# A decoder layer on one core: ScalarE's order in the expert steps, and who does the last sums and scalings

## The chip, the core and the metric

The kernel runs on one core of one Trainium2 chip. The core has TensorE (matrix products, results in PSUM), VectorE, ScalarE and GpSimd (elementwise work of different kinds), and SyncE, which does no arithmetic and issues transfers. Each engine runs its own queue in order; semaphores tie them. The metric is the device time of one execution in microseconds (us), taken as the median of several runs. Before the change it is 984.56 us (three runs, 982.49 to 984.77).

## The reference

A decoder layer in float32 with a layer norm behind each of three parts. The input has 8 sequences of 112 tokens with 512 features, so 896 tokens or seven tiles of 128.

```python
x = _layernorm(x + attn(x))             # causal self-attention, 16 heads of 128
x = _layernorm(x + xattn(x, ctx_2048))  # gated linear attention to 375 context rows
x = _layernorm(x + ffn(x))              # mixture of experts

# ffn: 8 experts, each token goes to its best two
logits = h @ router_weight.T + router_bias
top_vals, top_idx = jax.lax.top_k(logits, 2)
top_w = softmax(top_vals)
gate_up = h @ gate_up_proj + gate_up_proj_bias     # per expert, 512 -> 2 x 512
gate = minimum(gate_up[..., ::2], 7.0); up = clip(gate_up[..., 1::2], -7.0, 7.0)
act = (up + 1.0) * gate * sigmoid(1.702 * gate)
expert_out = act @ down_proj + down_proj_bias      # per expert, 512 -> 512
out = sum over the token's two experts of top_w * expert_out
```

## The kernel before

The first two thirds of the span (self-attention and cross-attention) are not touched. The change lies in the experts' part, the last `with` block, which starts near 740 us.

**Tokens in blocks.** The router (`route`) writes every token twice, once for each of its two experts, into an array `store` in memory, sorted by expert; `list_blocks` works out from the counts which expert and which block of `store` each of 18 steps gets. A step s takes a block of 128 rows (`xblk`, four buffers). Steps 0 to 4 have one expert each; steps 5 to 12 are paired, with 64 rows for each of two experts; steps 13 to 17 are again single. Weights lie in four lanes of three 1 MB slabs (gate, up, down). SyncE fetches the weights of a coming step when TensorE has released the slab, and skips the transfer where the lane already has that expert.

**A step in engines.** The loop over s at the end of the kernel issues, in an order written out by hand (`tc.manual_schedule` keeps the queues of TensorE, VectorE, ScalarE and SyncE as written), three stages at once:
- `project(s, st, 0)` and `project(s, st, 1)`: TensorE multiplies the turned block bT(s) by the gate and the up weights into PSUM (`gups`, L1143). VectorE adds the bias and clips (L1151, L1153, L1158). ScalarE computes the sigmoid of the gate (L1155). VectorE joins them to the gated block (L1159, L1162).
- `transposed_block` for aT(s-1) and, in `start(s + 1)`, for bT(s+1): TensorE turns the gated block of the step before and the token block of the step after into PSUM (L1040), ScalarE copies each into SBUF (L1044). `start` also has VectorE derive the per-row scalars (L1052 to L1078).
- `down(s - 1)`: TensorE multiplies aT(s-1) by the down weights (`yps`, L1170), and VectorE adds the result to a begun result y (L1181), which GpSimd scatters to an array `parts` in memory (L1183).

The begun result comes from `begin_result(s)`: ScalarE scales the down bias by the row's score (L1201) and the token block by a flag that says whether this is the row's first expert (L1202), GpSimd adds the two (L1203). The bias was spread over the partitions by VectorE's shuffle (`spread_biases`, L995) after a transfer that ScalarE issues (`fetch_biases`, L987). In the kernel before, shuffle and `begin_result(s + 1)` stand at the end of step s.

**The end.** A token's two results meet in two ways. For tiles of tokens, `close_tiles` adds the two halves read back from `parts` (L1235), takes layer-norm statistics, one root for all seven (`closing_roots`, L223 to L225), and scales each tile (`closing_scale`) before SyncE writes it out (L1244). The rows of the last five steps (`LATE` = 5, steps 13 to 17) come too late for that: each gathers the partner rows from `parts` into `sums` (L1210), adds its own result (`add_own`, L1206), is normed by `close_steps`, and is scattered into the output over the rows written before (`write`, L1220); `find_again` finds rows of which both halves fall into these steps. In the kernel before, `close_steps` takes steps 13 to 16 together and then step 17 alone, inside `finish`. `tick` and `settle` move `close_tiles` and the last tile's router work (`close`) along between the steps. L243 is the root of that tile's earlier layer norm, L530 and L533 its turning and copy for the router, L1265 the product in `find_again`.

Of the kernel before, what the change touches and what calls it, by code (L numbers as in the profile page):

```python
# [19 lines left out]
P = 128  # L20
# [40 lines left out]
def decoder_layer(ctx: ExitStack, tc: tile.TileContext, t_in: dict, out: bass.AP):  # L61
# [1058 lines left out]
    with tc.tile_pool(name="moe", bufs=2, reuse_waits="tile") as moe:  # L1120
# [17 lines left out]
        def project(s: int, st, k: int):  # L1138

            ps = bank(f"gups_{s}_{k}")  # L1140
            for c in range(C):
                for rows_, q in parts_of(s):
                    nc.tensor.matmul(  # L1143
                        ps[rows_],
                        st["bT"][:, c, rows_],
                        slab[3 * q + k][:, c, :],
                        start=(c == 0),
                        stop=(c == C - 1),
                    )
            a = moe.tile([P, I], F32, tag=f"gu{k}", name=f"gu_{s}_{k}", bufs=2 - k)  # L1150
            nc.vector.tensor_add(a, ps, st["bias"][:, k * I : (k + 1) * I])  # L1151
            if k == 0:
                nc.vector.tensor_scalar_min(a, a, LIMIT)  # L1153
                sg = moe.tile([P, I], F32, tag="sg", name=f"sg_{s}", bufs=1)
                nc.scalar.activation(sg, a, AF.Sigmoid, scale=ALPHA)  # L1155
                st["g"], st["sg"] = a, sg
            else:
                nc.vector.tensor_scalar(a, a, LIMIT, -LIMIT, ALU.min, ALU.max)  # L1158
                nc.vector.scalar_tensor_tensor(  # L1159
                    st["g"], st["g"], st["score"], st["sg"], ALU.mult, ALU.mult  # L1160
                )
                nc.vector.scalar_tensor_tensor(  # L1162
                    st["g"], a, 1.0, st["g"], ALU.add, ALU.mult
                )

        def down(s: int, st):
            ps = bank(f"yps_{s}", "aux")
# [34 lines left out]
            nc.scalar.activation(y, st["x"][:, :D], AF.Copy, scale=st["first"])  # L1202
            nc.gpsimd.tensor_add(y, y, bias)  # L1203

        def add_own(st):
            nc.vector.tensor_add(st["sum"], st["sum"], st["y"])  # L1206

        def gather(st):
            st["sum"] = sums[:, st["late"] * D : (st["late"] + 1) * D]
# [22 lines left out]
        def close_tiles():  # L1232
            for t in range(NT):
                engine = nc.vector if t < 4 else nc.gpsimd
                engine.tensor_add(xn[:, t, :], xn[:, t, :], seconds[:, t, :])  # L1235
                closing_stats(t, xn[:, t, :])
                if t in (1, 2):
                    yield
            yield
            closing_roots(0, NT)  # L1240
            yield
            for t in range(NT):
                closing_scale(t, xn[:, t, :], True)
                nc.sync.dma_start(out=out[t * P : (t + 1) * P, :], in_=xn[:, t, :])  # L1244

        def close_steps(*several, by_act=False):
            late = [(NT + s - (STEPS - LATE), steps[s]) for s in several]
# [35 lines left out]
        def finish(ps, st):  # L1283
            before_ = steps[STEPS - 2]
            nc.tensor.matmul(ps, st["same"], before_["y"], start=False, stop=True)
            nc.vector.tensor_add(st["sum"], st["sum"], ps)
            close_steps(STEPS - 1)

        def fetch_next(s: int, fetch):

# [8 lines left out]
        for s in range(STEPS + 1):  # L1299
            st = steps[s] if s < STEPS else None  # L1300
            before_ = steps[s - 1] if s else None
            if s == 0:
                spread_biases(0)
                begin_result(0)
            if st:
                project(s, st, 0)
                if s == 0:
# [1 line left out]
                    chains.append(close(NT - 1))  # L1309
                if s < STEPS - 1:  # L1310
                    tick()
            if s == STEPS:
                add_own(steps[s - 2])
            if before_:
                before_["aT"] = transposed_block(f"aT_{s - 1}", before_["g"], moe, "aT")
            if s == STEPS - 1:
                tick()
            if s == STEPS:
                settle(0)
                close_steps(*range(STEPS - LATE, STEPS - 1), by_act=True)  # L1320
            if s + 1 < STEPS:
                steps.append(start(s + 1, moe, "bT"))
                if s + 2 < STEPS:
                    fetch_biases(s + 2)
                if s + 1 > STEPS - LATE:
                    nc.vector.tensor_scalar_mul(diag, ident, keys[:, s + 1 : s + 2])
                if s == 2:
                    settle(0)
# [13 lines left out]
                find_again(s + 1)  # L1342
            if s + 1 < STEPS:
                spread_biases(s + 1)
                begin_result(s + 1)
            if s == STEPS - 1:
                settle(0)
                for late in steps[STEPS - LATE : STEPS - 2]:
                    add_own(late)

                add_own(st)
            if before_:
                down(s - 1, before_)
                if s == STEPS - 3:
                    chains.append(close_tiles())
                if s != STEPS - 3:
                    tick()
                if s == PAIRED:
                    for t in range(NT):
                        for k, to in ((1, xn), (0, seconds)):  # L1360
                            nc.sync.dma_start(
                                out=to[:, t, :],
                                in_=parts[k * T + t * P : k * T + (t + 1) * P, :],
                            )
                fetch_next(s - 1, fetch_down)
                if s + 3 < STEPS:
                    ahead_x.append(fetch_tokens(s + 3))
# [61 lines left out]
```

## Time and profile before

| | us |
|---|---|
| median of three runs | 984.56 |
| profiled execution, its own time | 981.93 |
| its span | 980.3 |
| TensorE busy | 921.4 (94%) |
| VectorE busy | 498.6 (51%) |
| ScalarE busy | 253.1 (26%) |
| GpSimd busy | 202.4 (21%) |

The profile is of one execution. Its lines are of several kinds. A timeline line gives start and duration in us, engine, line of the kernel, operation, tiles (out<-in) and shapes; brackets at its end give how long the engine stood before it and what released it. PE is TensorE, PEld its weight load, DVE VectorE, ACT ScalarE, POOL GpSimd, SP SyncE. In a line of the waits the three numbers are the total, how often, and the longest. Idle time of an engine that nobody waits for costs nothing.

### The profile page before, as it was taken

What the parts mean: (1) busy time and instruction counts of PE and PEld (TensorE: products, weight loads), DVE (VectorE), ACT (ScalarE), POOL (GpSimd) and SP (SyncE); (2) the same over time, 40 slices, a digit from 0 to 9 for tenths busy, and PEclk for the clock granted to TensorE, in tenths of its full rate; (3) what the DMA queues carried; (4) which work ended last, traced back from release to release, by engine and by line L of the source; (5) the groups of instructions that cost most, each with busy time, mean ns of one, the idle gap of its engine ahead of it and who ended that gap; (6) DMA issues with size and microseconds to landing.
All of it is one profiled execution on the core that took longest, in us unless ns stands there. A gap on an engine that the chain in (4) does not pass through costs nothing.

```text
span 980.3 us, 11063 instructions
## 1 busy us (share of the span) xinstructions
PE 921.4 (94%) x3915; PEld 467.8 (48%) x3915; DVE 498.6 (51%) x1116; ACT 253.1 (26%) x434; POOL 202.4 (21%) x264
## 2 busy tenths in 40 slices
PE   7998999999999999999999999997978799999974
PEld 3455644466445654654555455453444343334431
DVE  1356511145313551556421757666758755556685
ACT  1133311033102230322222233332214222222223
POOL 3133300031101221202002212221102422222152
PEclk9999999999999999999999999999969899999997
DMA  9995004102011001030100111113337899768953
GB/s 341 358 344 198 1 1 171 43 0 87 0 43 43 1 1 43 7 118 26 32 1 1 32 43 44 54 55 126 147 150 291 275 365 343 270 208 318 404 203 139
DMA packets 35063, 130.48 MB, mean 133 GB/s; under 512 B 3862, under 2 KB 8022, under 8 KB 25152
## 3 DMA queue, kind: packets, MB, share of 16 engines
q1 hardware_dynamic: 29296, 114.01, 32.1%
q0 software_dynamic: 4768, 14.98, 4.5%
q10 hardware_dynamic: 944, 0.79, 0.3%
q8 instruction: 31, 0.51, 0.2%
q14 instruction: 24, 0.20, 0.1%
HBM read 122.02 MB, written 30.06 MB: 155 GB/s over the span
## 4 chain that ended last, share of the span: by engine, by line
PE 78%; DVE 13%; issue 3%; ACT 3%; POOL 1%; DMA 1%; ACTq 0%; POOLq 0%; DVEq 0%
PE gups L1143 10%; PE ops L261 10%; PE vps L351 6%; PE yps L1170 5%; PE zps L459 3%; PE xqps L895 2%; PE xgps L895 2%; DVE z L868 2%; PE sps L411 2%; PE xops L261 2%; PE pps L451 1%; DVE p L436 1%; PE sumps L830 1%; PE aT_ps L1040 1%; DVE kf L790 1%
## 5 line engine op out<-in xcount | busy, mean ns | idle before, releaser
L1143 PE MATMUL gups<-slab,bT 128*64 128x512 f32 (+1 forms) x416 | 132.7, 601 | 0.0
L261 PE MATMUL ops<-slab,zT 128*128 128x512 f32 x224 | 97.9, 593 | 0.0
L1170 PE MATMUL yps<-slab,aT 128*64 128x512 f32 (+1 forms) x208 | 70.9, 624 | 10.6 <-ACT aT L1044 10.6
L1143 PEld LDWEIGHTS gups<-slab,bT 128*64 128x64 f32 (+1 forms) x416 | 47.8, 159 | 68.4 <-issue 68.3
L299 POOL TENSOR_TENSOR ws<-slab 128x256 f32<-128x256 f32 x16 | 11.7, 730 | 281.4 <-PE qk_5c L315 83.0
L261 PEld LDWEIGHTS ops<-slab,zT 128*128 128x128 f32 x224 | 42.0, 190 | 50.3 <-issue 49.5
L351 PE MATMUL vps<-slab,x0T 128*112 128x512 f32 x128 | 58.7, 613 | 1.0 <-DVE x0T L211 0.8
L1151 DVE TENSOR_TENSOR gu<-gups,biases 128x512 f32<-128x512 f32 x36 | 24.8, 689 | 62.8 <-PE gups L1143 62.8
L1170 PEld LDWEIGHTS yps<-slab,aT 128*64 128x64 f32 (+1 forms) x208 | 25.7, 167 | 49.7 <-issue 37.0
L268 DVE TENSOR_TENSOR xn<-xn,ops 128x512 f32<-128x512 f32 x28 | 19.2, 685 | 55.2 <-PE ops L261 55.2
L466 DVE COPY zT<-zps 128x448 f32<-128x448 f32 x32 | 20.0, 624 | 39.8 <-PE zps L459 39.8
L459 PEld LDWEIGHTS zps<-pT,v 112*128 112x128 f32 x256 | 33.5, 192 | 12.3 <-issue 11.2
L351 PEld LDWEIGHTS vps<-slab,x0T 128*112 128x112 f32 x128 | 22.9, 184 | 31.4 <-issue 29.7
L435 DVE TENSOR_REDUCE nm<-p 112x4 f32<-112x448 f32 x32 | 19.7, 615 | 30.6 <-POOL p L425 30.6
L261 PE MATMUL xops<-slab,gate 128*128 128x512 f32 x56 | 27.3, 633 | 7.1 <-DVE gate L870 7.1
L459 PE MATMUL zps<-pT,v 112*128 112x112 f32 x256 | 33.4, 273 | 0.0
L587 POOL DMA_INDIRECT store<-xn,rows x14 | 14.0, 1003 | 83.9 <-DVE count L627 60.1
L995 DVE STREAM_SHUFFLE biases<-biases 128x1024 f32<-128x1024 f32 (+1 forms) x28 | 29.8, 1099 | 0.0
L1183 POOL DMA_INDIRECT parts<-y,nums x16 | 16.8, 1049 | 60.9 <-DVE y L1181 44.6
L419 ACT ACTIVATE p<-sps 112x448 f32<-112x448 f32 x32 | 17.4, 544 | 45.6 <-PE sps L411 45.6
L411 PE MATMUL sps<-k,q 128*112 128x112 f32 x256 | 28.0, 262 | 0.0
L437 ACT ACTIVATE p<-p 112x448 f32<-112x448 f32 x32 | 18.4, 576 | 35.4 <-DVE p L436 35.4
(814 smaller groups left out, 1664.3 us busy)
## 6 DMA issues: line engine op xcount, KB each, us to landing
slab<-in_wg_dram SPq DMA_DIRECT2D x26, 1024.0 KB
slab<-in_wu_dram SPq DMA_DIRECT2D x26, 1024.0 KB
slab<-in_wd_dram SPq DMA_DIRECT2D x26, 1024.0 KB
store<-slab SPq DMA_DIRECT2D x8, 1806.0 KB
cT<-in_ctxT_dram SPq DMA_DIRECT2D x8, 750.0 KB
slab<-in_wq_dram SPq DMA_DIRECT2D x4, 1024.0 KB
slab<-in_wk_dram SPq DMA_DIRECT2D x4, 1024.0 KB
slab<-in_wo_dram SPq DMA_DIRECT2D x4, 1024.0 KB
```

The lines of the kernel that those rows point to most:

```text
L261: nc.tensor.matmul(ps, aT[:, c, t * P : (t + 1) * P], w[:, c, :], start=(c == 0), stop=(c == C - 1),)
L351: nc.tensor.matmul(ps[:S, :], xT[:, c, b * S : (b + 1) * S], w[:, c, :], start=(c == 0), stop=(c == C - 1),)
L411: nc.tensor.matmul(ps[:S, i * S : (i + 1) * S], qk["q"][:, rows], qk["k"][:, rows], start=True, stop=True,)
L435: nc.vector.tensor_reduce(nm, p, AX.X, ALU.max, negate=True)
L459: nc.tensor.matmul(zps[:, i * S : (i + 1) * S], v[:, half * 4 + i, hl * DH : (hl + 1) * DH], pT[:, i * S : (i + 1) * S], start=True, stop= ...
L466: nc.vector.tensor_copy(zT[:, hl, half * HALF : (half + 1) * HALF], zps[:, :HALF])
L868: nc.vector.reciprocal(zf, zf)
L895: nc.tensor.matmul(ps[:, :HALF], w[:, c, g * P : (g + 1) * P], xT[:, c, cols], start=(c == 0), stop=(c == C - 1),)
L995: nc.vector.stream_shuffle(b, b, [0] * XH)
L1143: nc.tensor.matmul(ps[rows_], st["bT"][:, c, rows_], slab[3 * q + k][:, c, :], start=(c == 0), stop=(c == C - 1),)
L1151: nc.vector.tensor_add(a, ps, st["bias"][:, k * I : (k + 1) * I])
L1170: nc.tensor.matmul(ps[rows_], st["aT"][:, c, rows_], slab[3 * q + 2][:, c, :], start=(c == 0), stop=(c == C - 1 and s < STEPS - 1),)
```

## The change

It has four parts.
1. In step s, ScalarE's copies of aT(s-1) and bT(s+1) are issued first, then the sigmoid (in a function of its own, `gate_sigmoid`), then `begin_result(s)`, which moves from the end of step s-1 into step s.
2. Of the late sums, those of steps 13 to 15 go to GpSimd; those of 16 and 17 stay on VectorE. They are issued after the down product of the step, and the sum of step 16 comes in step 17.
3. Of the seven tile scalings, the first three go to VectorE and four stay on ScalarE, and the generator `close_tiles` yields at other points, so that the root and the scalings come after step 17's second product.
4. `close_steps` takes steps 13 to 15 together, scaled by ScalarE, and in `finish` steps 16 and 17 together, scaled by VectorE.

```diff
             if k == 0:
                 nc.vector.tensor_scalar_min(a, a, LIMIT)
-                sg = moe.tile([P, I], F32, tag="sg", name=f"sg_{s}", bufs=1)
-                nc.scalar.activation(sg, a, AF.Sigmoid, scale=ALPHA)
-                st["g"], st["sg"] = a, sg
+                st["g"] = a
...
+        def gate_sigmoid(s: int, st):
+            sg = st["sg"] = moe.tile([P, I], F32, tag="sg", name=f"sg_{s}", bufs=1)
+            nc.scalar.activation(sg, st["g"], AF.Sigmoid, scale=ALPHA)
...
-        def add_own(st):
-            nc.vector.tensor_add(st["sum"], st["sum"], st["y"])
+        def add_own(st, engine=nc.vector):
+            engine.tensor_add(st["sum"], st["sum"], st["y"])
...
             yield
             closing_roots(0, NT)
-            yield
             for t in range(NT):
-                closing_scale(t, xn[:, t, :], True)
+                closing_scale(t, xn[:, t, :], t > 2)
                 nc.sync.dma_start(out=out[t * P : (t + 1) * P, :], in_=xn[:, t, :])
+                if t == 2:
+                    yield
+                    yield
...
             nc.vector.tensor_add(st["sum"], st["sum"], ps)
-            close_steps(STEPS - 1)
+            close_steps(STEPS - 2, STEPS - 1)
...
             if s == 0:
                 spread_biases(0)
-                begin_result(0)
...
-            if s == STEPS:
-                add_own(steps[s - 2])
             if before_:
                 before_["aT"] = transposed_block(f"aT_{s - 1}", before_["g"], moe, "aT")
-            if s == STEPS - 1:
-                tick()
+            if s + 1 < STEPS:
+                steps.append(start(s + 1, moe, "bT"))
+            if st:
+
+                gate_sigmoid(s, st)
+                begin_result(s)
             if s == STEPS:
                 settle(0)
-                close_steps(*range(STEPS - LATE, STEPS - 1), by_act=True)
+                close_steps(*range(STEPS - LATE, STEPS - 2), by_act=True)
             if s + 1 < STEPS:
-                steps.append(start(s + 1, moe, "bT"))
                 if s + 2 < STEPS:
                     fetch_biases(s + 2)
...
             if s + 1 < STEPS:
                 spread_biases(s + 1)
-                begin_result(s + 1)
+            if before_:
+                down(s - 1, before_)
             if s == STEPS - 1:
-                settle(0)
                 for late in steps[STEPS - LATE : STEPS - 2]:
-                    add_own(late)
+                    add_own(late, nc.gpsimd)
+                add_own(before_)

                 add_own(st)
             if before_:
-                down(s - 1, before_)
                 if s == STEPS - 3:
                     chains.append(close_tiles())
```

## The prediction

> **What bounds the kernel now.** I read the shares of the span first, then the waits of TensorE from 740 us on, then the timeline around each wait, then busy time and DMA share by stretch.
>
> ```profile
> PE 921.4 (94%) x3915; PEld 467.8 (48%) x3915; DVE 498.6 (51%) x1116; ACT 253.1 (26%) x434; POOL 202.4 (21%) x264
> ```
>
> TensorE sets the time, so an edit pays only where TensorE stands, or after its last matmul. From 740 us on it stands at five places. The timeline of TensorE alone gives them, with the wait and its releaser in brackets:
>
> ```profile
> 746.87 0.63 PE L530 MATMUL x2T_ps<-ident,xn 128*128 128x128 f32 x4 [2.93 <-DVE is_first L1054]
> 774.63 6.17 PE L1170 MATMUL yps<-slab,aT 128*128 128x512 f32 x8 [6.92 <-ACT aT L1044]
> 940.18 0.46 PE L1265 MATMUL keys<-sums,allones 128*128 128x128 f32 x2 [1.99 <-DVE sums L1326]
> 954.35 6.77 PE L1170 MATMUL yps<-slab,aT 128*128 128x512 f32 x8 [2.96 <-ACT aT L1044]
> 962.28 3.70 PE L1170 MATMUL yps<-slab,aT 128*128 128x512 f32 x8 [0.73 <-ACT aT L1044]
> ```
>
> The largest (6.92 us) ends with ScalarE's copy of a turned block. Its cause stands in the timeline of 758 to 785 us:
>
> ```profile
> 763.24 0.60 PE L1040 MATMUL aT_ps<-ident,gu 128*128 128x128 f32 x4
> ...
> 770.52 0.72 ACT L1201 ACTIVATE more_biases<-more_biases,score 128x512 f32<-128x512 f32 x1 [10.73 <-DVE more_biases L995]
> ...
> 772.09 1.60 DVE L1054 TENSOR_TENSOR is_first<-xblk,es 128x1 f32<-128x1 f32 x1
> 772.18 1.28 ACT L1155 ACT_TABLE_LOAD   x1 [0.33 <-DVE gu L1153]
> ...
> 774.01 0.57 ACT L1044 COPY aT<-aT_ps 128x512 f32<-128x512 f32 x1
> ...
> 775.76 0.69 DVE L1162 SCALAR_TENSOR_TENSOR gu<-gu,gu 128x512 f32<-128x512 f32 x1
> ```
>
> The block was turned in PSUM at 763.84. ScalarE stood for 10.73 us in front of a bias scaling that waits for a VectorE shuffle, then did two scalings, a table load and a sigmoid, and only then the copy. The stall also costs clock, as busy time by stretch shows (five pairs of busy time and count, then granted clock, share of the transfer engines, GB/s):
>
> ```profile
> 760.00:780.00 20.00, 13.08 (x31) 5.86 (x30) 17.08 (x68) 5.54 (x8) 7.16 (x10) 0.83 0.78 261
> 780.00:800.00 20.00, 20.00 (x60) 9.64 (x59) 8.88 (x23) 4.52 (x8) 6.48 (x8) 1.00 1.01 383
> 800.00:860.00 60.00, 60.00 (x277) 22.16 (x277) 34.44 (x79) 14.63 (x25) 16.22 (x19) 1.00 0.87 299
> 860.00:903.00 43.00, 42.95 (x197) 16.68 (x194) 24.14 (x62) 11.70 (x20) 11.49 (x12) 1.00 0.71 265
> ```
>
> In the trace's clock rows half clock stood from 773.4 to 780.2 and from 954.3 to 961.1: straight after the stalls of 6.92 and 2.96 us, so that eight matmuls took 6.17 and 6.77 us where they take 3.43 elsewhere.
>
> The end is set otherwise:
>
> ```profile
> 967.63 1.03 POOL L1220 DMA_INDIRECT out_dram<-sums,places  x1 [11.19 <-ACT sums L232]
> ...
> 973.08 0.99 POOL L1220 DMA_INDIRECT out_dram<-sums,places  x1 [0.30 <-issue]
> ```
>
> Five scattered writes leave GpSimd 1.35 us apart from the moment the first late sum is scaled; landing and closing take from 974.07 to 980.3.
>
> **The change, part by part.** s is the step; gate(s) and up(s) are its two products.
>
> *Order on ScalarE.* It was: bias scaling and result start of s (waiting for the shuffles that end step s-1), sigmoid(s), copy aT(s-1), copy bT(s+1), bias transfers. It becomes: both copies, sigmoid, the two scalings, transfers. No instruction is added, and one table load less is issued.
>
> (a) Around 744 us. The last tile's root (L243, at 745.65) stood behind the sigmoid's table load of step 0. Now its own load comes first, without a wait, on an idle engine, and it runs when its variance is there (VectorE's aggregate ends 743.59): 2.0 us earlier. TensorE waited 2.93 us for that tile. Its copy (L533) is now behind bT, load, sigmoid and two scalings: 743.95 + 0.57 + 1.28 + 0.63 + 0.72 + 0.71 = 747.9, done at 748.5, and TensorE needs it at 748.9, after gate(1). That product hides it; uncovered, each us costs one. I take 1.9.
>
> (b) The stall at 774. aT(1) is copied as soon as it is turned, so the down product follows up(2) at once: at 765.6 (767.5 less the 1.9 of (a)). It ends 769.1 at full clock, gate(3) at 772.5. What is late next is VectorE, which makes the block for the following turn. Its L1162 ended at 776.45: 1.9 earlier by (a), and 0.8 by L1054, which took 1.60 us beside GpSimd's begun result instead of 0.15. (1.45 would be won, but then the sigmoid, whose load still starts with L1153's end at 772.11 and which ends 1.99 later, comes last.) So the turn starts at 773.75 instead of 784.08: 6.92 + 2.74 (clock) + 1.9 - a new wait of 1.25 = **10.3 us**.
>
> The rule on this in the Trainium skill ("TensorE: Matmul & The Clock Gate", section "HAM oscillation — how this bites in real kernels") is to avoid idle gaps above about 3.4 us. By it the new waits of about 1 us are free and so would be waits of 3 us. The row says otherwise: 2.96 us at 954 was enough for half clock, while 2.93 us at 746 was not. By the rule a later stall of 3 us costs 3; by the row up to 3 + 3.2. I take the rule for waits near 1 us, and keep the row for the range.
>
> (c) What a faster TensorE triggers. The weights of the paired steps were loaded in a stream that is nearly full: share 1.01 and then 0.87 in the rows above (780 to 860 us: 383 and 299 GB/s). In the trace's transfer records 1 MB blocks followed one another every 3.4 us while they queued. Counting by 3.4 from the first one after the lists (771.23, now 769.2), the twentieth, a down weight of step 7, lands at 769.2 + 19 x 3.4 + 3.7 = 837.5. It was needed at 846.12; 10.3 us earlier is 835.8: late by 1.7. Its neighbours are met within 1 us. Bounds: at 3.2 us per block nothing is late; at 3.5 (from 808 to 827 us the pace was 3.6) it is 3.6, and with half clock behind it 6.8. I take **-2**: the pace of the longer stretch, and two short waits rather than one. From step 10 on most pair weights are skipped (share 0.71) and no further debt arises.
>
> Bias transfers are issued some 0.9 us later in the step, behind two scalings of 0.72 and 0.71 (the copies start about 0.5 earlier). SyncE waits for their landings (17.4 us in three waits at L962), so weights start up to 0.9 later; the smallest lead there, 3.0 us (down weight of step 8: landed 854.6, needed 857.6), covers it.
>
> (d) The end, with the times of before. GpSimd's result start no longer meets VectorE's L1153 (0.84 us beside it, 0.43 otherwise): VectorE, and with it the keys product, 0.4 earlier. aT(16) is copied at once: the stall of 2.96 and the half clock behind it (6.77 for 3.43) go, and the product before the last ends at 954.6. But VectorE's last gated block is ready only at 955.3 (its first add, behind the tiles' statistics, at 951.6, then 0.67 + 0.43 + 0.68 + 0.43 + 0.74 + 0.69), and its copy now stands behind sigmoid, two scalings, load and root: 953.4 + 0.7 + 0.7 + 1.28 + 0.3 = 956.4, done 957.0. The last product then ends at 960.7 instead of 966.0. Only part of that reaches the end, since VectorE goes on: block ready 955.3, root's two small steps until 956.9, three tile scalings x 0.55 (L234's row) = 958.6, result and two sums x 0.68 = 960.7, three statistics x 0.8 = 963.1, root and two small ones 963.9, ScalarE's first scaling 964.7. First write 964.7 instead of 967.63; the last two sums, closed in a pair, are ready by 968.2, before the fourth write at 968.8. All five writes move together: **3.0 us**, the 0.4 included.
>
> The two sums that wait on GpSimd: 1.28 us each (L1235's row there) against 0.69 on VectorE. Its four gathers end at 956.0, so sums and last start are done by 959.9 and VectorE needs them at 960.0. A rule speaks against this: "GPSIMD Engine Reference", section "Engine selection", keeps two-input elementwise work on VectorE, as GpSimd is about twice slower; the rows agree (1.28 to 0.69), but by the rule this costs 1.8 us more, by the timeline nothing as long as GpSimd only waits. Bounds 0 to 2 (its port meets VectorE's statistics).
>
> The scalings moved to VectorE take 3 x 0.55 from it and give ScalarE 3 x 0.72; counted above. The order on SyncE's queue is unchanged. GpSimd now writes parts of s-1 before it starts s: up to 2.7 us earlier for step 12's, hidden.
>
> Sum: 10.3 - 2 + 3.0 = 11.3. The profiled execution has a span of 980.3 and 981.93 in all; it would become 969.0 and 970.6. The median of the runs, 984.56, lies 2.6 above it: **973.3**.
>
> **Rivals.**
> 1. *The weights become the wait.* For: share 1.01. A late block of 3.6 us with half clock behind it takes 6.8 instead of 2: gain 6.5, 978.1. Against: the share of 0.87 and 0.71 after 800.
> 2. *The end gives nothing*: GpSimd's sums or the root ahead of the last copy hold VectorE by 3 us. Gain 8.3, 976.3. Against: GpSimd stands 11.19 us before the writes.
> 3. *No change*: the shift is eaten whole before step 9 and the end gives nothing. 984.5. Against: three stalls are removed in three places.
> 4. *Slower: ScalarE blocked by its bias transfers.* A transfer waits for the one that used its semaphore before, often a weight (a wait of 6.2 us at L1201 is put down to such a one). Now scalings and triggers stand directly ahead of the next copy. From a trigger to the next copy are 7.8 us, and the copy has 2.8 us of lead (843.36 + 0.57 against 846.12, and 0.6 earlier): blocking above 10.6 us stops TensorE. Over 13 steps it eats 11.3 from 11.5 us per step; at 12.5 per step it is -24.7 + 11.3: 998. Against: the longest such wait is 6.2.
>
> **How the numbers follow.** Forecast 0.60 (973.3, its own range 970 to 976), rival 1 0.18, rival 2 0.08, rival 3 0.05, rival 4 0.09. A measurement of this kernel tells some 0.3% (3 us) from nothing. Faster 0.86, same 0.05, slower 0.09. Range 969 to 979: no late block and the end as counted is 971.3, less some 2 for the spread of the runs; above, rival 1 and 1 us.
>
> **What would show it.** (a) The root at about 743.7. (b) The down product near 765.6 without half clock behind it, the turn near 774; if aT is copied early and the turn still starts after 780, the VectorE step is wrong. (c) Waits of TensorE for weights between 815 and 850, together near 2 us; above 4 rival 1 holds. (d) Last product about 5 us nearer to the one before, first write 3 us earlier against TensorE's step 17. Waits of ScalarE for transfers above 10 us would mean rival 4.

## The result, and the profile after

The changed kernel takes 978.37 us (median; 977.49 to 980.17) where the kernel before takes 983.72 on the same chip (982.49 to 984.77): ratio 0.9948, 95% interval 0.9933 to 0.9963. It is 5.35 us faster. (The 984.56 given ahead is the median of three of the five runs of the kernel before.) The forecast was 973.3, a gain of 11.3: the sign is right, and the gain is a little under half of what was summed.

The profiled execution has a span of 976.5 us (before: 980.3). The part of the program in front of 738 us is the same in both, and in this execution it happens to end 1.3 us later (first product of the last cross-attention output at 737.79 instead of 736.47). So 1.3 is added below wherever a time after is set against one before. Line numbers are those of the changed kernel; behind L1155 they are shifted (GpSimd's addition in the begun result, L1203, is L1205 now, the late sums L1208, the tile additions L1237).

The timeline of TensorE from 738 us on, with its waits, of the changed kernel (start, duration, in brackets the wait and what ended it):

```profile
746.05 0.63 PE L530 MATMUL x2T_ps<-ident,xn 128*128 128x128 f32 x4 [0.79 <-DVE is_first L1054]
774.98 0.63 PE L1040 MATMUL aT_ps<-ident,gu 128*128 128x128 f32 x4 [1.22 <-DVE gu L1160]
824.34 3.22 PE L1143 MATMUL gups<-slab,bT 128*64 128x512 f32 x13 [1.21 <-DMA slab<-in_wu_dram]
840.58 3.65 PE L1172 MATMUL yps<-slab,aT 128*64 128x512 f32 x14 [0.21 <-DMA slab<-in_wd_dram]
935.14 0.77 PE L1269 MATMUL keys<-sums,allones 128*128 128x128 f32 x2 [2.52 <-DVE sums L1330]
952.34 3.70 PE L1172 MATMUL yps<-slab,aT 128*128 128x512 f32 x8 [0.68 <-ACT aT L1044]
957.79 1.12 PE L1289 MATMUL yps<-y,sums 128*128 128x512 f32 x2 [1.75 <-DVE y L1183]
```

The waits of 6.92 at 774 and 2.96 at 954 are gone, the one at 746 has shrunk from 2.93 to 0.79. New are two waits for weights (824 and 840), a longer one at the `keys` product (2.52, before 1.99), and one of 1.75 before the last product. Where the old stall stood, the timeline of all engines after shows:

```profile
763.05 0.58 ACT L1044 COPY aT<-aT_ps 128x512 f32<-128x512 f32 x1 [4.09 <-PE aT_ps L1040]
766.72 3.60 PE L1172 MATMUL yps<-slab,aT 128*128 128x512 f32 x8
...
771.39 1.28 ACT L1166 ACT_TABLE_LOAD   x1 [7.27 <-DVE gu L1153]
772.69 0.63 ACT L1166 ACTIVATE sg<-gu 128x512 f32<-128x512 f32 x1
```

ScalarE copies aT at 763.05, straight after the turning, and the down product follows at 766.72 in 3.60 us, at full clock. Busy time by stretch (the columns are those of the prediction):

```profile
760.00:780.00 20.00, 18.78 (x56) 9.01 (x56) 17.57 (x71) 6.81 (x11) 7.73 (x10) 1.00 0.81 287
...
800.00:860.00 60.00, 58.58 (x268) 22.24 (x264) 31.50 (x71) 12.61 (x23) 16.05 (x19) 1.00 0.89 324
...
925.00:951.00 26.00, 23.48 (x62) 10.95 (x61) 23.93 (x51) 6.32 (x10) 12.15 (x11) 0.93 0.54 194
```

In 800 to 860 TensorE now has 58.58 of 60 us, with the transfers at 0.89 of their time. In 925 to 951 VectorE has 23.93 of 26 and hardly a gap, while TensorE waits and runs part of its time at half clock (0.93). What it does there and just behind, beside GpSimd:

```profile
928.45 0.99 POOL L1185 DMA_INDIRECT parts<-y,nums  x1 [0.86 <-DMA seconds<-parts]
929.07 1.95 DVE L1153 TENSOR_SCALAR gu<-gu 128x512 f32<-128x512 f32 x1
929.45 1.28 POOL L1237 TENSOR_TENSOR xn<-xn,seconds 128x512 f32<-128x512 f32 x1
...
951.90 2.50 POOL L1208 TENSOR_TENSOR sums<-sums,y 128x512 f32<-128x512 f32 x2
951.91 3.73 DVE L225 SCALAR_TENSOR_TENSOR closing<-closing 128x7 f32<-128x7 f32 x1
954.34 1.27 POOL L1205 TENSOR_TENSOR y<-y,biases 128x512 f32<-128x512 f32 x1
955.68 1.46 DVE L234 TENSOR_SCALAR xn<-xn,closing 128x512 f32<-128x512 f32 x3
...
963.99 1.03 POOL L1222 DMA_INDIRECT out_dram<-sums,places  x1 [8.38 <-ACT sums L232]
...
969.25 0.98 POOL L1222 DMA_INDIRECT out_dram<-sums,places  x1 [0.30 <-issue]
```

Two lines of the kernel before, for comparison:

```profile
936.95 1.26 DVE L1235 TENSOR_TENSOR xn<-xn,seconds 128x512 f32<-128x512 f32 x1
...
956.17 0.17 DVE L225 SCALAR_TENSOR_TENSOR closing<-closing 128x7 f32<-128x7 f32 x1
```

L225 works on 128x7 numbers and takes 0.17 us in the kernel before. Here it takes 3.73: from the start of the first of three GpSimd additions (two late sums and a begun result) to the end of the third. L1153, the clip of the gate, takes 1.95 where a scatter of GpSimd ends and an addition follows; alone it takes 0.43. In the kernel before L1153 took 0.84 beside the begun result, and a tile addition of VectorE (L1235) met GpSimd's: 1.26 instead of 0.68. The first scattered write starts at 963.99 (before 967.63), the last at 969.25 (973.08).

How the changed kernel gets from the end of L225 (955.64) to that write, the chain of work that ended last tells (start, duration, what):

```profile
955.68 2.94 ACT xn L232 x4
...
959.46 3.52 DMA out_dram<-xn
...
963.99 0.37 POOL out_dram L1222
```

Behind L225 it does not go through VectorE's sums and statistics. ScalarE scales its four tiles, SyncE writes the tiles out, the seventh lands at 962.98, and 1.0 us later GpSimd starts the first scattered write, which goes over the same rows. VectorE's own branch comes close: the first late sum is scaled at 963.06. Where that branch is the last one (kernel before, copies_alone and sums_on_vector below) the write starts 0.28 after it, which here would be 963.34. In the other eleven profiles the write starts 1.0 to 1.1 after the landing of the seventh tile.

The lead of the changed kernel over the one before tells where the time went. With the 1.3 it is 10.4 us at the turn of aT(2) (774.98 against 784.08) and still at step 7's gate product (817.36 against 826.43). It is 8.0 at the gate product of step 8 (831.25 against 837.91), 6.7 at that of step 9 (844.02 against 849.38), 6.9 at that of step 16 (924.71 against 930.29), and 5.1 at the last write:

| stretch | forecast | lead won or lost, us |
|---|---|---|
| to 775: root of the last tile, copy, clock | +10.3 | +10.4 |
| weights, step 7 | -2 | -3.7 |
| steps 9 to 15 | 0 | +0.2 |
| gate product of step 16 to the end of the span | +3.0 | -1.8 |
| sum | +11.3 | +5.1 |

### The profile page after: what moved, and what is told of

Same layout as the page of the kernel before. It is cut to its first block, busy times and chain, and to the rows that moved or that the text cites. A ratio compares the mean times of both kernels' runs of the same rounds, so it can differ in the third digit from the quotient of the medians.

```text
span 976.5 us, 11044 instructions
## 1 busy us (share of the span) xinstructions
PE 920.5 (94%) x3915; PEld 467.9 (48%) x3915; DVE 502.6 (51%) x1117; ACT 247.3 (25%) x429; POOL 206.1 (21%) x267
## 5 line engine op out<-in xcount | busy, mean ns | idle before, releaser
L1172 PE MATMUL yps<-slab,aT 128*64 128x512 f32 (+1 forms) x208 | 68.2, 601 | 0.9 <-ACT aT L1044 0.7
L1044 ACT COPY aT<-aT_ps 128x512 f32<-128x512 f32 x18 | 10.5, 585 | 133.5 <-PE aT_ps L1040 133.4
```

What stands on the lines that cost most here:

```text
L1172: nc.tensor.matmul(ps[rows_], st["aT"][:, c, rows_], slab[3 * q + 2][:, c, :], start=(c == 0), stop=(c == C - 1 and s < STEPS - 1),)
```

## Experiments

Theory: the head went as forecast; what is missing went into two terms. The weights of step 7 are late by more than 2 us because their stream is full. And from step 16 on the end is set by VectorE's queue, which stands still while GpSimd works, so that the additions given to GpSimd cost VectorE what they take. Rivals: the weights are late because they are issued late, behind bias transfers; the end is held by something else (the root's table, the gathers, TensorE), and GpSimd's additions are free.

Each of the four sets is of one chip, with medians of 982.23, 983.01, 982.86 and 983.18 for the kernel before. The last column is read from the profiles: from the start of step 16's gate product to the end of the span. It is of one execution each, and the two of the changed kernel differ by 1.4 us (51.8 and 53.2).

| kernel | median (range), us | ratio, 95% interval | step 16 to end, us |
|---|---|---|---|
| before | | 1 | 50.0 |
| changed kernel, first set | 978.37 (977.49 to 980.17) | 0.9948 (0.9933 to 0.9963) | 51.8 |
| *set 1:* copies_alone | 978.02 (977.23 to 978.92) | 0.9957 (0.9941 to 0.9973) | 50.9 |
| sums_on_vector | 976.63 (975.70 to 978.06) | 0.9942 (0.9925 to 0.9959) | 49.4 |
| biases_first | 980.26 (978.58 to 984.37) | 0.9976 (0.9966 to 0.9986) | 52.0 |
| one_weight_less | 976.67 (975.19 to 977.92) | 0.9935 (0.9919 to 0.9952) | 52.4 |
| *set 2:* after_again | 978.01 (977.59 to 979.81) | 0.9948 (0.9935 to 0.9961) | 53.2 |
| sums_and_scalings_back | 976.62 (975.33 to 977.54) | 0.9936 (0.9923 to 0.9948) | 49.9 |
| root_in_psum | 978.16 (976.57 to 980.75) | 0.9952 (0.9937 to 0.9967) | 52.7 |
| early_weight_less | 975.30 (973.99 to 981.36) | 0.9929 (0.9906 to 0.9952) | 52.1 |
| *set 3:* down_weight_later | 977.98 (977.38 to 980.73) | 0.9952 (0.9935 to 0.9968) | 51.7 |
| down_later_and_end_back | 977.78 (975.09 to 981.37) | 0.9942 (0.9920 to 0.9964) | 51.5 |
| no_tiles_on_gpsimd | 976.26 (974.96 to 979.27) | 0.9934 (0.9913 to 0.9955) | 51.1 |
| *set 4:* four_statistics_twice | 980.04 (977.94 to 983.02) | 0.9969 (0.9955 to 0.9983) | 53.8 |

### Part 1 alone

```diff
 (kernel before)
-                sg = moe.tile([P, I], F32, tag="sg", name=f"sg_{s}", bufs=1)
-                nc.scalar.activation(sg, a, AF.Sigmoid, scale=ALPHA)
...
+            if s + 1 < STEPS:
+                steps.append(start(s + 1, moe, "bT"))
+            if st:
+                gate_sigmoid(s, st)
+                begin_result(s)
             if s == STEPS - 1:
                 tick()
```

> The kernel before with part 1 alone (copies ahead of the sigmoid and the begun results); late sums, tile scalings and the closing of the last steps as before. Theory: from step 16 on VectorE's queue sets the end, and the edits of parts 2 to 4 give it nothing, because it stands still while GpSimd adds. The stall at 774 is gone as in the changed kernel, the weights are late as there, and the first scattered write comes within 1 us of its 963.99. About 978.5, within 1 us of the changed kernel. Rival (the forecast's term (d)): the edits at the end are worth 2.6 of the 3.0 us, so this one is at 981.

It took 978.02, ratio 0.9957; the changed kernel's interval (0.9933 to 0.9963) holds that. Its head is that of the changed kernel (turn of aT at 774.51, same wait of 1.2), and from step 16's gate product to the end it takes 50.9 us, where the two executions of the changed kernel take 51.8 and 53.2. So part 1 alone carries the gain, and parts 2 to 4 add nothing that can be measured. Here L1153 of step 16 happened to meet no addition of GpSimd (0.43, beside a scatter that began at 929.24), and L225 met one addition (0.83).

### The late sums back on VectorE

```diff
                 for late in steps[STEPS - LATE : STEPS - 2]:
-                    add_own(late, nc.gpsimd)
+                    add_own(late)
```

> The changed kernel with the three late sums back on VectorE. Theory: the sums on GpSimd cost VectorE what they take. The root's small step L225, 3.73 us beside three GpSimd adds, then meets one add alone (the begun result) and takes about 1.4; the 2.4 us go into three sums of 0.65. Same time as the changed kernel within 0.7 us, 978. Rival (sums on GpSimd are free, L225 is slow for another reason, such as the root's table or a transfer): L225 stays at 3.7 and VectorE has 2.0 us more to do, 980.4.

The timeline of this kernel:

```profile
951.33 1.28 POOL L1205 TENSOR_TENSOR y<-y,biases 128x512 f32<-128x512 f32 x1
951.75 0.90 DVE L225 SCALAR_TENSOR_TENSOR closing<-closing 128x7 f32<-128x7 f32 x1
...
954.66 3.09 DVE L1208 TENSOR_TENSOR sums<-sums,y 128x512 f32<-128x512 f32 x5
...
962.03 1.03 POOL L1222 DMA_INDIRECT out_dram<-sums,places  x1 [9.41 <-ACT sums L232]
```

L225 takes 0.90 beside the one addition that is left. VectorE does five sums in 3.09 us instead of two in 1.29, and still the first write comes 36.96 us after step 16's gate product, where the changed kernel needs 39.28. The time is 976.63, at or below the changed kernel's. The rival (980.4, L225 at 3.7) has fallen: for VectorE's queue the sums were not cheaper on GpSimd.

### What holds L225

The fast kind in the text that follows is the instruction that takes 0.43 us for 128x512 numbers from SBUF to SBUF (the clips), where VectorE's additions and statistics of that size take 0.66 to 0.69.

```diff
+        by = rstd
+        if a == 0:
+            by = bank("root_ps")[:, : b - a]
+            nc.vector.reciprocal(by, rstd)
         nc.vector.reciprocal(rstd, rstd)
         nc.vector.scalar_tensor_tensor(
-            closing[:, 3, a:b], closing[:, 0, a:b], -1.0, rstd, ALU.mult, ALU.mult
+            closing[:, 3, a:b], closing[:, 0, a:b], -1.0, by, ALU.mult, ALU.mult
         )
```

> The changed kernel with one more reciprocal of 128x7 that writes to PSUM, so that the tiles' L225 reads one operand from SBUF and one from PSUM instead of two from SBUF. It tells what holds L225 for 3.73 us. Theory (VectorE stands only where an instruction reads two operands from SBUF or is of the fast kind, while GpSimd adds): L225 takes 0.2 beside the same three GpSimd adds, ScalarE's four scalings start 3 us earlier, and VectorE's own scalings (L234) stand instead, until GpSimd is done; time as before, 978. Rival (any VectorE instruction stands, or L225 waits for something else): L225 keeps its 3.7 us.

L225 is L229 here, and the scalings are L236 (ScalarE) and L238 (VectorE):

```profile
952.22 2.51 POOL L1212 TENSOR_TENSOR sums<-sums,y 128x512 f32<-128x512 f32 x2
952.36 0.11 DVE L229 SCALAR_TENSOR_TENSOR closing<-closing,root_ps 128x7 f32<-128x7 f32 x1
952.50 2.93 ACT L236 ACTIVATE xn<-xn,closing 128x512 f32<-128x512 f32 x4
952.50 4.65 DVE L238 TENSOR_SCALAR xn<-xn,closing 128x512 f32<-128x512 f32 x3
954.67 1.28 POOL L1209 TENSOR_TENSOR y<-y,biases 128x512 f32<-128x512 f32 x1
```

With one operand in PSUM the same instruction takes 0.11 us beside the same additions, and ScalarE scales at once. VectorE's own three scalings, which read and write SBUF, stand in its place: 4.65 us where they take 1.46, until GpSimd is done, and the last tile goes out when it does in the changed kernel (959.48 and 959.46). The time is that of the changed kernel (978.16 and 978.01). So L225 did not stand for the root or its table, and not every instruction stands: in the changed kernel the statistics at 938.08 (L218) and the comparison at 938.90 (L1271, which reads the `keys` product in PSUM) keep their 0.69 and 0.66 beside GpSimd's addition of 938.32 to 939.59.

The Trainium skill has this as a rule ("SBUF — State Buffer", section "SBUF: two separate sides"): VectorE and GpSimd share a pair of ports, an instruction of VectorE in a fast two-port mode, or with two SBUF inputs beside a GpSimd instruction that reads SBUF, needs it, and whoever starts first has it for its whole instruction. The traces agree on which instructions stand, and for one addition on how long (0.83 to 1.31 for L225 beside 1.28). By the rule as it stands L225, which starts 0.01 us behind the first of three additions, would take an estimated 1.4; the measured 3.73 show that GpSimd's queued additions follow one another with VectorE still waiting. Nor did the first to start always have it: a clip that the profile starts 0.26 us ahead of GpSimd's first addition stood for 4.25 (four_statistics_twice, below). The measurement decides: the price is the whole group.

### The sums and the scalings back

```diff
             closing_roots(0, NT)
+            yield
+            yield
             for t in range(NT):
-                closing_scale(t, xn[:, t, :], t > 2)
+                closing_scale(t, xn[:, t, :], True)
...
-                if t == 2:
-                    yield
-                    yield
...
-                    add_own(late, nc.gpsimd)
+                    add_own(late)
```

> The changed kernel itself, so that the next three can be compared with it on one chip: 0.995 of the kernel before. Theory and rival agree.

> The changed kernel with the late sums on VectorE and all seven tile scalings on ScalarE behind its last copy (parts 2 and 3 undone, part 4 and the copies kept). Theory: VectorE's queue, without a gap from step 16 on, sets the end; the sums there cost as little as on GpSimd (L225 0.9 instead of 3.73), and three scalings of 0.49 leave the queue. First scattered write 3 us earlier than the changed kernel's, counted from the gate product of step 16 (36.3 instead of 39.3 after it), unless the seven writes of tiles, the last issued about 33 after it and landing 3 later, hold it at 36.5. 974.8 to 975.5 where the changed kernel has 978. Rival (the edits at the end are good and only GpSimd's luck was bad): VectorE has 2.0 of sums more and 1.5 of scalings less, so the same as the changed kernel, 978 to 979.

The changed kernel took 978.01 in this set. With parts 2 and 3 undone it takes 976.62, and each of its times (975.33 to 977.54) lies below each of the changed kernel's (977.59 to 979.81), though the intervals of the ratios overlap. Of the kernels that load all weights it is the only one that stands apart from the changed one, by 1.4 us; 2.5 to 3.2 were expected. The first write came 37.1 us after step 16's gate product (39.3), where 36.3 to 36.5 was expected. L1153 of step 16 met GpSimd again (1.98), and L225 took 1.31. VectorE's branch would still have let the write start at 36.4 (first sum scaled at 960.67, and 0.28); but with all seven scalings on ScalarE the last tile landed only at 960.62, and the write started 1.0 behind it, at 961.63.

The second profiled execution of the changed kernel (the longest of its five runs) adds something. TensorE had no half clock behind the `keys` wait there and came 1.6 us earlier to step 17 (from the gate product of step 16: 14.07 against 15.62), and yet the end came 1.4 later, because the tile addition of step 16 met GpSimd:

```profile
936.90 0.97 POOL L1185 DMA_INDIRECT parts<-y,nums  x1 [6.00 <-DVE gu L1157]
937.54 2.19 DVE L1237 TENSOR_TENSOR xn<-xn,seconds 128x512 f32<-128x512 f32 x1
937.90 1.27 POOL L1205 TENSOR_TENSOR y<-y,biases 128x512 f32<-128x512 f32 x1
...
952.40 0.63 PE L1040 MATMUL aT_ps<-ident,gu 128*128 128x128 f32 x4 [2.42 <-DVE gu L1160]
```

That addition (L1237, 0.68 alone) took 2.19, and the turn of the last block waited 2.42 us for VectorE. An earlier TensorE gained nothing there.

### Tiles added on VectorE

```diff
 (down_later_and_end_back, shown below)
-                engine = nc.vector if t < 4 else nc.gpsimd
+                engine = nc.vector
```

> The kernel before this one with the last three tile additions on VectorE too, so that GpSimd adds nothing in step 16 but the begun results. Theory (GpSimd's additions hold VectorE): L1153 of step 16 takes 0.43 instead of 1.9 and L1277 to L1279 of step 15 lose about 1, against three additions of 0.69: 0.5 us better, 973.5. Rival (what GpSimd does beside VectorE is free on average): 2.0 us worse, 976.

L1153 of step 16 fell to 0.43 and the `keys` wait to 0.99, as expected, but `again` (L1278, 128x4) met the begun result of step 17 in its place and took 1.74. The medians (976.26 against 977.78) differ by less than the ranges, which overlap: neither theory nor rival is shown.

### More work for VectorE

```diff
                 closing_stats(t, xn[:, t, :])
+                if t > 2:
+                    st = small.tile([P, 6], F32, tag="st", name=f"st_more_{t}")
+                    nc.vector.bn_stats(st, xn[:, t, :])
```

> The changed kernel with four more statistics of 128x512 on VectorE (0.69 each, of tiles 3 to 6, their results unused), in the stretch of 943 to 947 us, where TensorE is some 10 us ahead of the kernel before. They read one operand, so that GpSimd's additions do not hold them. Theory (VectorE's queue, without a gap from step 15 on, sets the end): the 2.7 us move everything behind them; the two adds of GpSimd that stood beside L225 are then partly over when VectorE comes to it, which may give back up to 1: 979.7 to 980.7 where the changed kernel has 978.0. Rival (TensorE, or the landing of gathers and tile writes, sets the end): no more than 0.5 us, 978.0 to 978.5.

980.04: 2.0 above the changed kernel of set 2, within the theory's 979.7 to 980.7; by the rival 978.0 to 978.5. The two are of different sets, and the intervals of their ratios just meet (0.9955 to 0.9983 and 0.9935 to 0.9961), so this speaks for VectorE's queue and does not prove it. Nor does it part the two branches behind L225: the statistics stand ahead of the root and delay both, the tile writes and VectorE's sums. In the profiled execution (983.02, the longest of eight) the three additions of GpSimd met another instruction, the clip of step 17, whose 0.43 became 4.25, while L225 took its 0.17:

```profile
954.01 4.25 DVE L1156 TENSOR_SCALAR gu<-gu 128x512 f32<-128x512 f32 x1
954.27 2.49 POOL L1208 TENSOR_TENSOR sums<-sums,y 128x512 f32<-128x512 f32 x2
956.71 1.26 POOL L1205 TENSOR_TENSOR y<-y,biases 128x512 f32<-128x512 f32 x1
```

### Why step 7's weights are late

```diff
 (one_weight_less; early_weight_less has i == 1)
+                lanes = sorted(todo[n])
+                if n == 6 and fetch is fetch_down:
+                    lanes = [i for i in lanes if i == 0]
+                fetch(n, lanes)
```

> The changed kernel, but one down weight of step 6 (the second lane's, 1 MB) is not loaded, so the product there uses the weight of an earlier step: this part of the computation is changed. Theory A (the stream is full): all later blocks land about 3.4 us earlier, TensorE does not wait in step 7, the lead of 9.1 us holds to step 9, and since the end is VectorE's from there on it follows whole: 978.4 - 3.6 = 974.8. Theory B (late issue behind bias transfers): the waits in step 7 stay in the main, 977.5 to 978.5.

> The changed kernel, but the other down weight of step 6 (its first lane's, 1 MB, the seventeenth block of the stream from 738 us on) is not loaded; this part of the computation is changed. In the run with the second lane's left out the block stood behind the late up weight, and only the wait in the down product went. Theory A (the stream is full): both late weights of step 7 land 3.4 us earlier, TensorE does not wait in step 7, and the whole 3.6 us is won: 974.5. Theory B (late issue): the waits stay in the main, over 977.

The first did not test what was written: the weight left out stands behind the late up weights in the queue (it is issued at 814, they from 805 to 809), so their wait stayed (1.34) and only the one in the down product went. Between the products that start at 751.66 and 844.02 in the changed kernel it gained 1.2 us. The second leaves out a weight that stands ahead of them. Of TensorE's waits, this is all that was left between the turn at 775 and the turn at 948:

```profile
775.37 0.63 PE L1040 MATMUL aT_ps<-ident,gu 128*128 128x128 f32 x4 [1.21 <-DVE gu L1160]
932.54 0.46 PE L1269 MATMUL keys<-sums,allones 128*128 128x128 f32 x2 [2.67 <-DVE sums L1333]
948.08 0.63 PE L1040 MATMUL aT_ps<-ident,gu 128*128 128x128 f32 x4 [0.90 <-DVE gu L1160]
```

Between the same two products it gained 3.5 us, and the median fell by 2.7 (975.30 against 978.01; five of its six runs lie at 973.99 to 975.82, below all of the changed kernel's, and one at 981.36): with 1 MB less ahead of them no weight of step 7 is late. The stream is full.

```diff
 (biases_first)
+                if s + 2 < STEPS:
+                    fetch_biases(s + 2)
             if st:
                 gate_sigmoid(s, st)
                 begin_result(s)
```

> The changed kernel with the bias transfers of step s+2 issued straight behind the two copies, ahead of the sigmoid and the begun result, about 1.5 us earlier. It tells why weights of step 7 are late (TensorE waits 1.2 us in its up product at 824.3 and 1.2 in its down product at 840.6; lead 9.1 before, 5.4 after). Theory A (the stream of weights is full): their landing does not move, TensorE waits as long, 978. Theory B (the weight transfer is issued late because SyncE waits for a bias transfer, as the chain shows for the down weight of step 7: bias landed at 829.66, weight issued at 829.77): the down weight lands about 1.5 earlier, its wait goes and 1.2 to 2 us are won, 976.5.

980.26, ratio 0.9976: slower than the changed kernel, and the down weight of step 7 was no earlier (wait of 1.05 at 841.46). The edit did not do what it was meant to: that weight was issued later, at 833.20 instead of 829.77. It answers the question all the same, since 3.4 us of later issue made the product that waits for it start only 0.9 later (841.46 against 840.58). What stands ahead in the stream decides, not the issue behind the bias transfers. The loss came from elsewhere: the sigmoid of step 2 started at 773.51 instead of 772.69, and the next turn waited longer:

```profile
775.80 0.68 PE L1040 MATMUL aT_ps<-ident,gu 128*128 128x128 f32 x4 [2.22 <-DVE gu L1160]
```

2.22 instead of 1.22, with half clock from 776.2 to 779.7 behind it, cost 2.7 us by the down product that follows. At 782.62 a sigmoid waited 4.67 us for bias transfers issued ahead of it: this is the kind of blocking that rival 4 spoke of; in the changed kernel the sigmoid there, at 778.48, waited for VectorE alone.

```diff
 (down_weight_later)
+                if s == EARLY - 1:
+                    late_down = s - 1
+                else:
+                    if s == EARLY:
+                        fetch_next(late_down, fetch_down)
+                    fetch_next(s - 1, fetch_down)
```

> The changed kernel with one transfer moved on SyncE's queue: the down weight of step 6 for its first lane, needed at 824.7 and landed at 809.4, is issued behind the four gate and up weights of step 7 instead of ahead of them. Theory A with order (the stream is full, and the up weights of step 7 stand behind a down weight that has time): the up weights land about 3.4 us earlier, at 819.3, and TensorE does not wait in the up product of step 7 (2.3 us in all); the two down weights of step 6 land at 822.7 and 825.4, which costs a new wait of about 0.7; the down weight of step 7 still lands at 838.5 and its wait stays. Of 3.6 us lost some 2 come back: 976 where the changed kernel has 978. Rival (the transfers are late for another reason than what stands ahead of them): no gain, 978.

> The same move, with the late sums back on VectorE and all tile scalings on ScalarE. Theory: the two gains add, since both shorten what stands on the path to the end: 2 from the weights and 1.4 to 3 from the end: 973.5 to 974.5, below both kernels. Rival (a TensorE that comes earlier to step 16 only waits longer for VectorE's queue, which has no gap from step 15 on): the weights' gain is lost, 976.6 as without the move.

The up product of step 7 no longer waits, as expected, but the waits moved into the down products of steps 6 and 7:

```profile
826.89 3.65 PE L1172 MATMUL yps<-slab,aT 128*64 128x512 f32 x14 [0.48 <-DMA slab<-in_wd_dram]
840.00 3.65 PE L1172 MATMUL yps<-slab,aT 128*64 128x512 f32 x14 [0.51 <-DMA slab<-in_wd_dram]
```

Both start on the weight that is there and come to the late one 1.5 us after their start (825.39 and 838.47). Up to the product at 844.02 (here 843.39) 0.65 us were won instead of 2: this stream, which owed some 3 us, was not paid off by another order. The time is the changed kernel's (977.98). With the end put back as well it is 977.78, not the sum of two gains; the tile addition of step 16 took 2.19 in that profile, as in the second execution of the changed kernel.

## Why the prediction was right and wrong

**(a) Right.** Said: the root at 743.7. It started at 744.83, less 1.3. The copy for the router behind it (748.67, less 1.3; said 747.9) held nothing up.

**(b) Right.** Said: turn of aT(2) at 773.75 with a new wait of 1.25. Measured: 774.98, less 1.3, with 1.22. No half clock followed that wait. The 10.3 became 10.4. One reading beside it was off: on the timeline's own zero the clock rows of the kernel before give half clock from 772.8 to 779.6 and from 953.7 to 960.6, 0.6 earlier than said. So it began inside the two stalls and not behind them; the last section comes back to this.

**(c) Right mechanism, term too small: -2 became -3.7.** The pace of 3.4 was near (counted at 128 packets of 8 KB each, 15 blocks start from 769.98 to 821.54: 3.44), but the step "its neighbours are met within 1 us" failed. The up weights of step 7 cost 2.4 us, and the down weight 1.3 more. In the chain of waits this down weight arrives at 840.53; by the count it is 837.5, or 838.8 with the 1.3: 1.7 too early. early_weight_less shows that 1 MB, some 3.4 us of stream, is what was missing. No half clock came with it, so rival 1 as written (6.8) did not occur, though its 978.1 is near the measured time. That is luck: most of the rest was lost at the end.

**(d) Wrong: +3.0 became -1.8.** The step that failed is the one that gave VectorE nothing to pay for GpSimd's additions. In three places:
- "GpSimd's result start no longer meets VectorE's L1153 ... 0.4 earlier." It does not, but without it in front the scatter of the step before and the tile addition behind that scatter moved 1.3 us earlier, into its place, and L1153 took 1.95 instead of the 0.43 counted: 1.5 us. I had moved that scatter ("up to 2.7 us earlier ... hidden") without asking what VectorE does when the next addition comes. Of the 1.5 some 0.6 came back by luck, as VectorE's tile addition no longer met GpSimd (0.67 instead of 1.26).
- GpSimd's sums "by the timeline nothing as long as GpSimd only waits. Bounds 0 to 2 (its port meets VectorE's statistics)." The statistics were not hit at all. The root's small step was, and it took 3.73 instead of 0.17: 3.6 us. The upper bound of 2 was too low for three additions in a row.
- The count from "block ready 955.3" to "first write 964.7" goes through VectorE's queue alone. It left these two out, and it has no term for the landing of the tile writes, which in the changed kernel holds the first scattered write for 0.65 us more.

Counted from step 16's gate product (930.29 before, 924.71 after), the first addition of step 17 was forecast at 21.3 and came at 22.25: 0.9 late. The root's small steps were to end at 26.6 and ended at 30.9: 4.3 late. The first write was to come at 34.4 and came at 39.3: 4.9 late. So L225 makes up 3.6 of the 4.9, what is left of L1153 0.8, and the stretch behind L225 the last 0.5. VectorE also stands for 1.13 us before the root's small steps, until ScalarE has loaded a table (1.28) and taken the root; that was in the forecast, and no run here took it away on its own.

Rival 2, "GpSimd's sums or the root ahead of the last copy hold VectorE by 3 us", named the right place; against the forecast the end was worse by 4.8 where it said 3, and its "against" (GpSimd stands 11.19 us before the writes) was about GpSimd, where the question was VectorE. Rival 4 did not occur: ScalarE's copies wait for TensorE alone.

The rule weighed ahead of (c), that gaps below some 3.4 us are free, held for the waits near 1 us on which the sum used it, and failed at the `keys` product (below).

## What to carry to other kernels

Before work goes to an idle engine, list what the other engine does at that very time. Here an addition on GpSimd was free for VectorE only beside instructions that read at most one operand from SBUF and are not of the fast kind: statistics (0.69), comparisons and additions with a PSUM operand (0.66 to 0.69). Move the queue whose end sets the time, follow it through the transfers behind it, and count the new lead of another engine as nothing: here TensorE was 9.9 us ahead at the last turn (951.07 against 960.95) and the end only 3.8. This transfer stream was full, and part of a stall taken out ahead of it (3.7 of 10.4 us) came back as a debt; bytes left out paid it, another order did not.

## What the runs showed of the hardware

VectorE instructions with two operands from SBUF, or of the fast kind, stood through a whole group of GpSimd additions, whatever their own size: 3.73 us for 128x7 (L225), 4.65 for three scalings that take 1.46 alone, 4.25 for a clip that takes 0.43.

GpSimd's scatters and gathers did not hold them. In the 14 profiles 77 clips and additions of VectorE from 738 us on ran beside a scatter or gather and no addition; 76 took their usual time and one clip 0.50. In the changed kernel, for example, the clip at 770.89 took 0.43 beside the scatter of 770.54 to 771.57, and the tile addition at 937.36 took 0.69 beside that of 936.89 to 938.29. It is the addition that follows: where one stood within 0.03 us behind a scatter or gather, VectorE instructions were held that the profile starts up to 0.5 us ahead of that addition, though not all (in four_statistics_twice the clip at 783.55 kept its 0.44, with an addition at 783.78). L1153 started at 929.07, the addition at 929.45; in early_weight_less they started at 926.33 and 926.85, and L1153 took 2.10. Whether the addition takes hold ahead of its recorded start, or the record is late, the traces do not tell.

The length of a wait alone does not decide on half clock, but the traces show what goes with it. The granted clock changed only on a raster of 3.41 us (in the changed kernel at 934.68, at 938.10 and, seven steps on, at 961.99). Laid over the wait at the `keys` product, the raster sorts all 14 profiles by how much of the wait fell into one of its intervals:

| profile | wait, us | most of it in one interval, us | half clock |
|---|---|---|---|
| biases_first, down_weight_later | 2.28, 2.57 | 2.28, 2.57 | yes |
| root_in_psum, sums_and_scalings_back | 2.40, 2.54 | 2.17, 2.14 | yes |
| changed kernel, sums_on_vector | 2.52, 2.02 | 2.06, 2.02 | yes |
| one_weight_less | 2.45 | 2.00 | yes |
| early_weight_less | 2.67 | 1.97 | no |
| before, down_later_and_end_back | 1.99, 2.62 | 1.88, 1.78 | no |
| after_again, copies_alone, four_statistics_twice | 2.40, 1.62, 2.54 | 1.69, 1.57, 1.56 | no |
| no_tiles_on_gpsimd | 0.99 | 0.99 | no |

The two waits over which the prediction stumbled fit: 2.96 at 954 had 2.34 in one interval, 2.93 at 746 was split into 1.57 and 1.36. This is an ordering found in the traces, not tried by a run, and the 2 us are no fixed threshold: near 720 us, and at the last products, 1.76 to 1.93 in one interval were enough. All of this lies below the 3.4 us of the rule.
